# A transformer block on one core: a new order of work ahead of the first attention scores

## The chip, the core and the metric

The kernel runs on one core of a Trainium2 chip. The core has five instruction streams that work side by side and wait for one another through semaphores: TensorE (PE: matrix products and turns, with its weight loads shown as PEld), VectorE (DVE), ScalarE (ACT), GpSimd (POOL) and SyncE (SP), which here only issues DMA transfers. A suffix q (SPq, ACTq) marks an engine's own instruction sequencer, for instance while it issues a transfer. The metric is the device time of one execution in microseconds (us).

## The reference

Two sequences of 1024 tokens of width 256 go through self-attention, cross-attention to 154 condition tokens of width 192, and a gated feed-forward layer, with 16 heads of width 64, all in float32. Each stage starts with a layer norm and ends with a residual sum:

```python
h = _layernorm(x, ln1_g, ln1_b)
x = _attention(h, h, sa_wq, sa_wk, sa_wv, sa_wo, sa_bo) + x
h = _layernorm(x, ln2_g, ln2_b)
x = _attention(h, cond_emb, ca_wq, ca_wk, ca_wv, ca_wo, ca_bo) + x
h = _layernorm(x, ln3_g, ln3_b)
p = h @ ff_w1 + ff_b1
a, gate = (p[..., :D_FF], p[..., D_FF:])
h = a * jax.nn.gelu(gate, approximate=False) @ ff_w2 + ff_b2
return h + x
```

The change touches the first layer norm of the first sequence, and the first queries and keys that are made from it.

## The kernel before

Work on the first sequence begins with its 1024 tokens as eight tiles of 128 (`NT` = 8). `tile_order` pairs tile i with tile 4 + i, so the order is 0, 4, 1, 5, 2, 6, 3, 7. `norm_pieces` gives four lists of functions. `stats(t)` (L235) runs BATCH_NORM_STATS2 and its aggregation on DVE for the t-th tile of that order. `deviation(t)` (L245) makes 1/sqrt(var + eps) for a pair: a sum on DVE (L248), a power on POOL (L252). `normalize(t)` (L255) makes `off` = -mean x rstd on DVE (L258) and then the normalized pair `xn`, one tile on ACT (L276) and one on POOL (L273). `turn(t)` (L279) turns the pair on TensorE into two PSUM banks `ph` (two turns in each) and returns `store` (L290), which copies four chunks into `hT` with the norm's gain and shift, chunks 0 and 1 on DVE (L297), chunks 2 and 3 on ACT (L301). Gain and shift are columns of `cols`, one value for each partition.

Engines take their instructions in the order in which the program text emits them, since everything is under `tc.manual_schedule()` (L1264). So the lines 1290 to 1313 are a schedule written out by hand. `emit` (L1268) calls pieces one behind another. `part(what, i)` (L1279) projects 128 tokens of each half of the sequence to queries or keys of the first two heads (`project_both`, L362); the two halves go to two PSUM banks at once. `take(what, i)` (L1284) copies 256 such columns for each half into the tiles `q_sa` and `k_sa`, the first half on ACT, the second on DVE (`take_both`, L375). The names `own` and `banks` are the two double banks that later hold the first scores; `first_k` are two more banks for the last keys. 27 turns of the identity matrix (L1290) stand ahead of the first work of TensorE.

Behind that, the loop at L1324 runs 128 steps `p`. A step makes scores for two groups of 64 queries of one half against all 1024 keys (`self_first`, L704, and `scores`, L519), takes row maxima on DVE (L712) and exponents on ACT (L537), exchanges statistics between partitions by DMA (L547), and takes other pieces from the list `work` (`run_work`, L601), whose copies out of PSUM are held in `stores` until `flush(stores)` is called. Step 0 reads query columns 0 to 127 of the first half, step 1 columns 128 to 255. The queries that the beginning leaves out are the first entry of `work` (L1321): `self_queries(..., P, 2 * P)`, columns 256 to 511 of each half. Their copies to `q_sa` are both on ACT (L384).

Loads are issued on SP and ACT in the order of the text (L105 to L177): x's eight tiles in four transfers of two tiles, then gain and shift of the first norm straight into columns (L110, 4-byte elements), then the weights (L134), the other norms' parameters as rows (L172), the condition and a bias. Those rows are turned to columns by `turn_rows` (L192) during step 4. The transfers share eight semaphores; a ninth transfer is issued once the one before it on its semaphore has landed.

The pool `ps_m` gives the banks of `mm_tile`, `ps_o` those of `sum_tile`, two each. `held_v` (L214) holds values of the attention from step 1 on; its plane 3 is written by `move_values` (L449), which the loop calls first at step 5.

Of the kernel before, what the change touches and what calls it, by code (L numbers as in the profile page):

```python
# [13 lines left out]
P = 128  # L14
# [4 lines left out]
def tile_transformer_block(ctx: ExitStack, tc: tile.TileContext, a: dict, out: bass.AP):  # L19
# [63 lines left out]
    def load_x(queue, b, t):  # L83

        queue.dma_start(
            out=xt[b, t // GT][:, t % GT:t % GT + 2, :],
            in_=x[b, t * P:(t + 2) * P, :].rearrange("(t p) d -> p t d", p=P),
        )
# [125 lines left out]
    held_v = const.tile([P, 4, NT, P], F32, tag="held_v", name="held_v")  # L214
# [8 lines left out]
    def norm_pieces(kind, b, first=False):  # L223
# [21 lines left out]
        def deviation(t):  # L245
            mv = st["mv", t]
            var = small.tile([P, 2], F32, tag="var", name=f"var_{ln}_{b}_{t}")
            (nc.vector if first else nc.gpsimd).tensor_scalar(  # L248
                var, mv[:, :, 1], EPS, 1.0, op0=ALU.add, op1=ALU.mult
            )  # L250
            rstd = small.tile([P, 2], F32, tag="rstd", name=f"rstd_{ln}_{b}_{t}")
            nc.gpsimd.tensor_tensor(rstd, var, power, ALU.pow)  # L252
            st["rstd", t] = rstd

        def normalize(t):  # L255
            rstd = st["rstd", t]
            off = small.tile([P, 2], F32, tag="off", name=f"off_{ln}_{b}_{t}")
            nc.vector.scalar_tensor_tensor(  # L258
                off, st["mv", t][:, :, 0], -1.0, rstd, op0=ALU.mult, op1=ALU.mult
            )  # L260
# [8 lines left out]
            for i in range(2):  # L269
                xs = xt[b, order[t + i] // GT][:, order[t + i] % GT, :]  # L270
                xs, own = xs.rearrange("p (c d) -> p c d", c=nh), xn[:, :, i, :]
                if not narrow(kind, b) or first and i == 1:
                    nc.gpsimd.tensor_scalar(  # L273
                        own, xs, rstd[:, i:i + 1], off[:, i:i + 1], op0=ALU.mult, op1=ALU.add)
                else:
                    nc.scalar.activation(  # L276
                        own, xs, AF.Identity, bias=off[:, i:i + 1], scale=rstd[:, i:i + 1])

        def turn(t):  # L279

            n = 2 if first else 1
            bank = mm_tile if first and t == 2 else spare["bank"]
# [6 lines left out]

            def store():  # L290
                k = NC * 2 * P // nh
                for c in range(nh):
                    own = st["hT"][:, c, t // 2 * k:(t // 2 + 1) * k]
                    turned = ph[c * n // nh][:, c % (nh // n) * k:][:, :k]
                    gain, shift = cols[:, g0 + c:g0 + c + 1], cols[:, b0 + c:b0 + c + 1]
                    if spare["turned"] or first and c < nh // 2:
                        nc.vector.tensor_scalar(  # L297
                            own, turned, gain, shift, op0=ALU.mult, op1=ALU.add
                        )
                    else:  # L300
                        nc.scalar.activation(own, turned, AF.Identity, bias=shift, scale=gain)  # L301

            return store
# [960 lines left out]
    with tc.manual_schedule():  # L1264
# [19 lines left out]
        def take(what, i):  # L1284
            at = banks[what] if i < 2 else banks["k2"]
            take_both(qk["sa", 0, 0]["qk".index(what)], at, scale if what == "q" else None,
                      i * P, 2 * P, shared=True)


        for _ in range(27):  # L1290
            nc.tensor.transpose(own[0][:, 1, :P], ident, ident)
# [243 lines left out]
```

## Time and profile before

| what | value |
|---|---|
| time, median of 3 runs | 1073.81 us (1072.66 to 1074.61) |
| the profiled execution's own time | 1075.05 us |
| its span, first to last instruction | 1073.2 us |
| instructions | 48628 |
| granted TensorE clock, mean | 1.000 |
| DMA moved | 60.95 MB, mean 57 GB/s |

A row of the chain or the timeline begins with its start and its length in us. In groups and timelines there follow the engine, the line of the kernel (L526), the operation, and output<-input by the program's names; x32 is the number of instructions. A bracket at the end tells how long the engine was idle before and what it waited for. In a row of waits stands who waited for whom, the total in us, the number of times and the longest. A row of one tile's instructions has the shortest, median and longest duration in ns and the first and last start.

### The profile page before, as it was taken

The page shows a single profiled execution, that of the slowest core. Times are in us where ns is not written, and L with a number is a line of the kernel's source. Part 1 is how long each engine was busy: PE and PEld are TensorE (multiplying, and loading weights), DVE is VectorE, ACT ScalarE, POOL GpSimd, SP SyncE. Part 2 cuts the span into 40 slices and gives each one's busy share as a digit, 9 for nine tenths or more (in the row PEclk, how much of TensorE's full clock was granted, in tenths as well). Part 3 has the DMA queues.
Part 4 walks back from the last instruction along what each step waited for, and adds up shares of the span by engine and source line. Part 5 has one row for each costly group of instructions (what it writes and reads, how often), then busy time and mean ns, then how long its engine had stood idle before and what let it go on. Part 6 is the DMA issues. An engine that isn't in the chain of part 4 may idle for free.

```text
span 1073.2 us, 48628 instructions
## 1 busy us (share of the span) xinstructions
PE 1059.4 (99%) x20196; PEld 716.2 (67%) x20196; DVE 883.1 (82%) x1321; ACT 646.9 (60%) x2096; POOL 777.0 (72%) x1652
## 2 busy tenths in 40 slices
PE   8999999999999999999999999999999999999998
PEld 6566777556556555555665665466766667788998
DVE  5789899998989989999999899968777887655554
ACT  5766677677666666676777666665566564342231
POOL 2677777778777777677777777776666876499884
PEclk9999999999999999999999999999999999999999
DMA  3132122121021121111111101125776545000000
GB/s 101 38 73 54 29 68 53 25 63 41 22 59 25 34 51 34 39 34 34 44 22 45 44 14 38 36 59 139 164 177 172 123 108 114 16 6 15 21 10 30
DMA packets 86045, 60.95 MB, mean 57 GB/s; under 512 B 32122, under 2 KB 74562, under 8 KB 85826
## 3 DMA queue, kind: packets, MB, share of 16 engines
q1 hardware_dynamic: 84450, 57.07, 22.1%
q8 instruction: 159, 2.61, 1.1%
q10 hardware_dynamic: 1376, 0.79, 0.2%
q14 instruction: 60, 0.49, 0.2%
HBM read 27.91 MB, written 2.10 MB: 28 GB/s over the span
## 4 chain that ended last, share of the span: by engine, by line
PE 74%; DMA 7%; SPq 6%; POOL 6%; DVE 2%; issue 2%; ACT 1%; POOLq 0%; DVEq 0%; ACTq 0%
PE s L526 14%; PE po L578 13%; DMA st<-st 7%; SPq L547 6%; PE py_ca L500 5%; PE py_sa L500 4%; PE poc L951 4%; PE pq_ca L369 4%; PE pq_sa L369 4%; PE pb L1072 4%; PE pk_sa L369 4%; PE pq L1217 3%; PE pv_sa L405 3%; POOL p L650 3%; PE sc L871 2%; PE pa L1072 2%
## 5 line engine op out<-in xcount | busy, mean ns | idle before, releaser
L650 POOL TENSOR_SCALAR p<-p,rd,ee 128x512 f32<-128x512 f32 x512 | 391.9, 771 | 80.0 <-DVE rd L640 79.6
L537 ACT ACTIVATE p<-s,st 128x512 f32<-128x512 f32 x512 | 345.5, 687 | 169.7 <-DVE st L712 164.5
L712 DVE TENSOR_REDUCE st<-s 128x2 f32<-128x1024 f32 x256 | 308.6, 1206 | 56.8 <-issue 17.3
L675 DVE STREAM_TRANSPOSE pT<-p 128x1024 f32<-128x1024 f32 x256 | 302.8, 1219 | 1.5 <-POOL p L650 1.2
L526 PE MATMUL s<-k_sa,q_sa 64*32 64x512 f32 x4096 | 257.8, 591 | 2.8 <-ACT p L537 2.0
L578 PE MATMUL po<-pT,held_v 64*32 64x256 f32 x8192 | 240.8, 376 | 0.7 <-DVE pT L675 0.6
L578 PEld LDWEIGHTS po<-pT,held_v 64*32 64x32 f32 x8192 | 182.5, 106 | 67.0 <-issue 26.0
L526 PEld LDWEIGHTS s<-k_sa,q_sa 64*32 64x32 f32 x4096 | 89.7, 106 | 93.1 <-issue 46.6
L888 ACT ACTIVATE p<-sc,neg 128x154 f32<-128x154 f32 x256 | 96.4, 405 | 78.9 <-DVE rden L896 75.0
L899 POOL TENSOR_SCALAR p<-p,rden 128x154 f32<-128x154 f32 x256 | 97.3, 406 | 51.8 <-DVE rden L896 51.5
L537 ACT ACTIVATION_READ_ACCUMULATOR p<-s,st 128x1 f32 x512 | 104.0, 203 | 0.0
L555 POOL TENSOR_TENSOR dd<-st 128x8 f32<-128x8 f32 x128 | 26.0, 203 | 82.4 <-DMA st<-st 80.6
L500 PE MATMUL py_sa<-sa_wo,o_sa 128*128 128x256 f32 x256 | 59.7, 386 | 1.0 <-ACT held_v L415 1.0
L500 PE MATMUL py_ca<-ca_wo,o_ca 128*128 128x256 f32 x256 | 60.2, 383 | 0.0
L877 DVE TENSOR_REDUCE neg<-sc 128x6 f32<-128x924 f32 (+1 forms) x48 | 47.8, 996 | 14.9 <-PE sc L871 14.9
L369 PE MATMUL pq_ca<-hT_ln,ca_wq 64*64 64x512 f32 (+1 forms) x544 | 59.1, 590 | 0.9 <-DMA ca_wq<-in_L_xattn_ca_wq_dram 0.8
L500 PEld LDWEIGHTS py_sa<-sa_wo,o_sa 128*128 128x128 f32 x256 | 47.3, 190 | 19.0 <-issue 5.2
L369 PE MATMUL pq_sa<-hT_ln,sa_wq 64*32 64x512 f32 (+1 forms) x976 | 57.8, 586 | 0.7 <-ACT held_v L415 0.7
L369 PE MATMUL pk_sa<-hT_ln,sa_wk 64*32 64x512 f32 x960 | 57.1, 590 | 0.2 <-ACT q_sa L384 0.2
L888 ACT ACTIVATION_READ_ACCUMULATOR p<-sc,neg 128x1 f32 x256 | 56.5, 221 | 0.0
L915 DVE STREAM_TRANSPOSE pT_ca<-p 128x480 f32<-128x480 f32 (+1 forms) x96 | 52.9, 587 | 0.9 <-POOL p L899 0.8
L405 PE MATMUL pv_sa<-sa_wv,hT_ln 64*32 64x256 f32 x1792 | 52.9, 376 | 0.0
(158 smaller groups left out, 1476.0 us busy)
## 6 DMA issues: line engine op xcount, KB each, us to landing
wf<-pT_ca SPq DMA_DIRECT2D x128, 128.0 KB, 2.4
st<-st SPq DMA_DIRECT2D x512, 1.0 KB, 2.0
held_v<-held_v SPq DMA_DIRECT2D x32, 256.0 KB, 4.0
sa_wq<-in_L_xattn_sa_wq_dram SPq DMA_DIRECT2D x32, 128.0 KB, 2.8
sa_wk<-in_L_xattn_sa_wk_dram SPq DMA_DIRECT2D x32, 128.0 KB, 3.6
sa_wv<-in_L_xattn_sa_wv_dram SPq DMA_DIRECT2D x16, 256.0 KB, 4.2
ca_wq<-in_L_xattn_ca_wq_dram SPq DMA_DIRECT2D x32, 128.0 KB, 3.1
wf<-in_L_xattn_ff_w_dram SPq DMA_DIRECT2D x12, 256.0 KB
```

The source lines that it names most:

```text
L369: nc.tensor.matmul(pq[r][f:f + m, at:at + n], lhsT=wt[own, c, f:f + m], rhs=h[own, c, t0:t0 + n], start=(c == 0), stop=(c == NH - 1), tile ...
L405: nc.tensor.matmul(pv[r][f:f + KB, e * VC:(e + 1) * VC], lhsT=h[half, c, t0:t0 + KB], rhs=wt[half, c, :], start=(c == 0), stop=(c == NH - ...
L500: nc.tensor.matmul(py[:, e * D:(e + 1) * D], lhsT=o[:, i, (t + e) * P:(t + e + 1) * P], rhs=wo[kind][:, g * HP + i, :], start=(i == 0), st ...
L526: nc.tensor.matmul(sc[a4 * KB:(a4 + 1) * KB, j, :], lhsT=q[r, c:c + KB], rhs=k[r, h * HB:(h + 1) * HB], start=True, stop=True, tile_positi ...
L537: nc.scalar.activation(pr[:, j, :], sc[:, j, :], AF.Exp, bias=st[:, 0, 0, i, j:j + 1], accum_out=st[:, 0, 1, i, j:j + 1],)
L578: nc.tensor.matmul(po[a2][d:d + KB, :QH // 2], lhsT=v[e][r, t, d:d + KB], rhs=pT[r, d // DH * NK + n, :], start=(t == 0 and e == 0), stop= ...
L650: nc.gpsimd.tensor_scalar(pr[:, j, :], pr[:, j, :], own["rd"][:, c:c + 1], own["ee"][:, 0, c:c + 1], op0=ALU.mult, op1=ALU.mult,)
L675: nc.vector.transpose(halves[h][:, :, c:c + KB], slots[p]["p"][i].rearrange("p j (n k) -> p (j n) k", k=KB))
L712: nc.vector.tensor_reduce(st[:, 0, 0, i, :], sc[i], AX.X, ALU.max, negate=True)
L888: nc.scalar.activation(pr_[:, j, i, :T], sc[:, j, i * T:(i + 1) * T], AF.Exp, bias=neg[:, j, i:i + 1], accum_out=den[:, j, i:i + 1],)
L899: nc.gpsimd.tensor_scalar(pr_[:, j, i, :T], pr_[:, j, i, :T], rden[:, j, i:i + 1], 1.0, op0=ALU.mult, op1=ALU.mult,)
L1072: nc.tensor.matmul(into[:, :BT], lhsT=lhs, rhs=wh[pair][i], start=first, stop=True, skip_group_check=True)
```

## The change

It does these things, all ahead of the scores of step 1.

- x's first four tiles are loaded as single tiles, then gain and shift of the first norm as eight rows (in a plane of `held_v` that isn't used yet, hence the earlier allocation), then x's last four tiles in two transfers.
- The eight rows are turned by TensorE and copied to `cols` on ACT.
- In the first norm, `off` is made by POOL from a negated mean that DVE makes. Of the second pair both tiles are normalized on POOL.
- Statistics stand ahead of the chunk copies in DVE's order; `turn` returns a function that copies one chunk on the engine named, and the list tells which. Turns 0 and 2 use the banks of `sum_tile`, turns 1 and 3 those of `mm_tile`.
- 20 turns of the identity instead of 27 ahead, and 5 more behind turn 0.
- All four key parts go to one bank for each half; of the queries, part 0 alone is made ahead of the first scores, and `self_queries` makes columns 128 to 511 behind them. Their copies are flushed at the end of step 0.

```diff
-    def load_x(queue, b, t):
+    def load_x(queue, b, t, n):
         queue.dma_start(
-            out=xt[b, t // GT][:, t % GT:t % GT + 2, :],
-            in_=x[b, t * P:(t + 2) * P, :].rearrange("(t p) d -> p t d", p=P),
+            out=xt[b, t // GT][:, t % GT:t % GT + n, :],
+            in_=x[b, t * P:(t + n) * P, :].rearrange("(t p) d -> p t d", p=P),
         )
...
-    for t in range(0, NT // 2, 2):
-        load_x(nc.sync, 0, t)
-        load_x(nc.scalar, 0, NT // 2 + t)
-    for n in names[:2]:
-        for r0 in range(0, P, HR):
-            (nc.scalar if n == names[0] else nc.sync).dma_start(
-                out=cols[r0:r0 + HR, row_of[n]:row_of[n] + NH],
-                in_=w[n].rearrange("(r p) -> p r", p=HR),
-            )
+    for t in range(2):
+        load_x(nc.sync, 0, t, 1)
+        load_x(nc.scalar, 0, NT // 2 + t, 1)
+    held_v = const.tile([P, 4, NT, P], F32, tag="held_v", name="held_v")
+    rows1 = held_v[:n_cols, 3, 0, :]
+    for n, queue in zip(names[:2], (nc.scalar, nc.sync)):
+        own = rows1[row_of[n]:row_of[n] + NH, :]
+        for f in range(0, P, HR):
+            queue.dma_start(out=own[:, f:f + HR], in_=w[n].rearrange("(r p) -> r p", p=HR))
+    load_x(nc.sync, 0, 2, 2)
+    load_x(nc.scalar, 0, NT // 2 + 2, 2)
...
             st["rstd", t] = rstd
+            if first:
+                neg = small.tile([P, 2, 4], F32, tag="zz", name=f"neg_{ln}_{b}_{t}")[:, 0, :2]
+                nc.vector.tensor_scalar(neg, mv[:, :, 0], -1.0, 1.0, op0=ALU.mult, op1=ALU.mult)
+                off = st["off", t] = small.tile([P, 2], F32, tag="off", name=f"off_{ln}_{b}_{t}")
+                nc.gpsimd.tensor_tensor(off, neg, rstd, ALU.mult)
...
-                if not narrow(kind, b) or first and i == 1:
+                if not narrow(kind, b) or first and (i == 1 or t == 2):
                     nc.gpsimd.tensor_scalar(
...
-            bank = mm_tile if first and t == 2 else spare["bank"]
+            bank = mm_tile if first and t % 4 == 2 else spare["bank"]
...
+            def store_chunk(c, vector):
+                k = NC * 2 * P // nh
+                own = st["hT"][:, c, t // 2 * k:(t // 2 + 1) * k]
+                turned = ph[c * n // nh][:, c % (nh // n) * k:][:, :k]
+                gain, shift = cols[:, g0 + c:g0 + c + 1], cols[:, b0 + c:b0 + c + 1]
+                if vector:
+                    nc.vector.tensor_scalar(own, turned, gain, shift, op0=ALU.mult, op1=ALU.add)
+                else:
+                    nc.scalar.activation(own, turned, AF.Identity, bias=shift, scale=gain)
...
         def part(what, i):
-            at = banks[what] if i < 2 else banks["k2"]
-            project_both(at, wsl["sa", 0, what], hT["sa", 0], P, i * P, P, i % 2 * P)
+            project_both(banks[what], wsl["sa", 0, what], hT["sa", 0], P, i * P, P, i * P)
...
-        for _ in range(27):
-            nc.tensor.transpose(own[0][:, 1, :P], ident, ident)
-        emit(stats[0], stats[1], deviation[0])
-        emit(stats[2], stats[3], normalize[0], deviation[1], stats[4], normalize[1])
-        copies = [turn[0](), turn[1]()]
-        copies[0]()
+        warm(own[0][:, 1], 20)
+        emit(stats[0], stats[1], deviation[0], stats[2], normalize[0], stats[3], deviation[1], stats[4])
+        nc.tensor.transpose(own[1][:, 0, :n_cols], rows1, ident[:n_cols, :n_cols])
+        nc.scalar.copy(cols[:, :n_cols], own[1][:, 0, :n_cols])
+        turned = [turn[0]()]
+        warm(own[0][:, 1], 5)
+        chunks(turned[0], (0,), (1, 2, 3))
+        emit(normalize[1])
         part("q", 0)
+        turned.append(turn[1]())
         part("k", 0)
-        emit(stats[5], deviation[2])
-        copies[1]()
-        emit(stats[6], normalize[2], stats[7], deviation[3])
-        copies = turn[2]()
-        part("q", 1)
+        emit(stats[5], deviation[2], stats[6])
+        chunks(turned[1], (), (2, 3))
+        emit(normalize[2], stats[7], deviation[3])
+        chunks(turned[1], (0, 1), ())
+        turned.append(turn[2]())
+        part("k", 1)
         emit(normalize[3])
-        copies()
-        part("k", 1)
-        copies = turn[3]()
-        banks["k2"] = two_banks("first_k")
+        chunks(turned[2], (0, 1), (2, 3))
+        take("q", 0, 1)
+        turned.append(turn[3]())
         part("k", 2)
-        copies()
-        take("q", 0)
-        take("k", 0)
+        chunks(turned[3], (0, 1), (2, 3))
         part("k", 3)
-        take("k", 2)
+        take("k", 0, 2)
+        take("k", 2, 2)
...
-        work.append(costing(2, lambda: self_queries(*units[0], P, 2 * P)))
+        work.append(costing(2, lambda: self_queries(*units[0], P, P)))
...
+            if p == 0:
+                flush(stores)
```

`chunks(store_chunk, vector, scalar)` calls the copy of each chunk of its first list on DVE, then of its second list on ACT; `warm(bank, n)` turns the identity n times; the third argument of `take` is the number of 128-column blocks.

More of the change, by code (lines that the diff above doesn't have):

```diff
@@ L213, in tile_transformer_block @@
     ends = const.tile([P, DA // 2], F32, tag="ends", name="ends")
-    held_v = const.tile([P, 4, NT, P], F32, tag="held_v", name="held_v")
     hT, vs, qk, oT = {}, {}, {}, {}
@@ L253, in deviation @@
             st["rstd", t] = rstd
+            if first:
[3 more added lines that the diff above has]
+                nc.gpsimd.tensor_tensor(off, neg, rstd, ALU.mult)
         def normalize(t):
             rstd = st["rstd", t]
[L257 to L260, printed above, removed]
+            if first:
+                off = st["off", t]
+            else:
+                off = small.tile([P, 2], F32, tag="off", name=f"off_{ln}_{b}_{t}")
+                nc.vector.scalar_tensor_tensor(
+                    off, st["mv", t][:, :, 0], -1.0, rstd, op0=ALU.mult, op1=ALU.mult
+                )
             if narrow(kind, b) and not first:
@@ L288, in turn @@
                     st["xn", t][i], ident)
+            def store_chunk(c, vector):
[5 more added lines that the diff above has]
+                    nc.vector.tensor_scalar(own, turned, gain, shift, op0=ALU.mult, op1=ALU.add)
+                else:
+                    nc.scalar.activation(own, turned, AF.Identity, bias=shift, scale=gain)
             def store():
-                k = NC * 2 * P // nh
                 for c in range(nh):
[L293 to L303, printed above, removed]
+                    store_chunk(c, spare["turned"])
+            return store_chunk if first else store
         return (
@@ L1279, in part, with take @@
         def part(what, i):
-            at = banks[what] if i < 2 else banks["k2"]
-            project_both(at, wsl["sa", 0, what], hT["sa", 0], P, i * P, P, i % 2 * P)
-        def take(what, i):
-            at = banks[what] if i < 2 else banks["k2"]
+            project_both(banks[what], wsl["sa", 0, what], hT["sa", 0], P, i * P, P, i * P)
+        def take(what, i, n):
+            at = [bank[:, i * P:] for bank in banks[what]]
             take_both(qk["sa", 0, 0]["qk".index(what)], at, scale if what == "q" else None,
-                      i * P, 2 * P, shared=True)
@@ L1290, in tile_transformer_block, with chunks @@
-        for _ in range(27):
-            nc.tensor.transpose(own[0][:, 1, :P], ident, ident)
-        emit(stats[0], stats[1], deviation[0])
-        emit(stats[2], stats[3], normalize[0], deviation[1], stats[4], normalize[1])
-        copies = [turn[0](), turn[1]()]
-        copies[0]()
+                      i * P, n * P, shared=True)
+        def chunks(store_chunk, vector, scalar):
+            for c in vector:
+                store_chunk(c, True)
+            for c in scalar:
+                store_chunk(c, False)
@@ new lines, in warm @@
+        def warm(bank, n):
+            for _ in range(n):
+                nc.tensor.transpose(bank[:, :P], ident, ident)
+        warm(own[0][:, 1], 20)
[5 more added lines that the diff above has]
+        chunks(turned[0], (0,), (1, 2, 3))
```

## The prediction

> **What bounds the kernel now.** I read the page's busy row and chain first, then what TensorE waits for (whole span, and 17 to 80 us), and then only the beginning.
>
> ```profile
> PE 1059.4 (99%) x20196; PEld 716.2 (67%) x20196; DVE 883.1 (82%) x1321; ACT 646.9 (60%) x2096; POOL 777.0 (72%) x1652
> ...
> PE 74%; DMA 7%; SPq 6%; POOL 6%; DVE 2%; issue 2%; ACT 1%; POOLq 0%; DVEq 0%; ACTq 0%
> ...
> PE first L1291 <- POOL ident masks.py:199: 1.9, 1, 1.9
> PE ph_ln L286 <- POOL xn_ln L273: 1.5, 5, 0.8
> ...
> PE s L526 <- DVE k_sa L390: 0.6, 1, 0.6
> PE pk_sa L369 <- ACT q_sa L384: 0.2, 1, 0.2
> ```
>
> TensorE is busy 1059.4 of 1073.2 us. The last two rows are all that it waits for between 17 and 80 us. So a microsecond counts only if TensorE's own sequence reaches the same instruction earlier; what other engines gain is worth nothing. Now the beginning: the chain, TensorE's timeline, and busy time per stretch (the first figure is its length, the second TensorE's):
>
> ```profile
> 1.91 6.02 PE first L1291 x27
> 7.93 0.45 PE ph_ln L286 x4
> ...
> 15.09 2.03 PE first_k L369 x32
> ...
> 17.71 1.95 PE s L526 x32
> 19.67 1.93 PE pq_sa L369 x16
> 21.59 0.67 PE pc L203 x8
> ...
> 22.19 1.96 PE L526 MATMUL s<-k_sa,q_sa 64*32 64x512 f32 x32
> ...
> 22.19:49.00 26.81, 26.81 (x426) 14.91 (x425) 19.34 (x21) 20.35 (x63) 14.82 (x33) 1.00 0.13 31
> ```
>
> Up to 7.7 us TensorE turns the identity. First scores (p=0) start at 17.71, those of p=1 at 22.19; from there TensorE is busy 26.81 of 26.81 us, and the change alters nothing behind it. **The ruler is therefore the start of p=1's scores, 22.19 us**, not that of the first scores.
>
> **The change part by part.** *x and the first statistics.*
>
> ```profile
> 4.33 0.43 DVE L242 BATCH_NORM_STATS2 st_ln<-x 128x6 f32<-128x256 f32 x1 [4.33 <-DMA x<-in_x_dram]
> ...
> 4.89 0.40 DVE L242 BATCH_NORM_STATS2 st_ln<-x 128x6 f32<-128x256 f32 x1
> ...
> 5.53 0.17 DVE L248 TENSOR_SCALAR var_ln<-mv_ln 128x2 f32<-128x2 f32 x1
> ...
> 5.78 0.71 POOL L252 TENSOR_TENSOR rstd_ln<-var_ln,power 128x2 f32<-128x2 f32 x1 [3.93 <-DVE var_ln L248]
> 6.92 0.56 POOL L273 TENSOR_SCALAR xn_ln<-x,rstd_ln,off_ln 128x256 f32<-128x256 f32 x1 [0.43 <-DVE off_ln L258]
> ...
> GB/s 0 19 141 378 386 127 65 213 233 231 231 83 8 104 198 192 87 0 0 0 0 0 0 0 18 1 1 1 149 115 10 1 138 126 1 18 0 0 0 0
> ...
> SPq L134 <- DMA x<-in_x_dram: 1.8, 2, 1.5
> 4.64 1.26 SPq L134 DMA_DIRECT2D sa_wq<-in_L_xattn_sa_wq_dram  x2
> ```
>
> The GB/s row (window 0 to 40 us) has one figure per microsecond: 0.16 MB had moved by 3 us, 378 KB/us follow. The first two loads (0.51 MB) were through at about 3.9; statistics began at 4.33 and SP's wait for x ended at 4.64, so landing lags by 0.4 to 0.7. With single tiles the first pair (0.26 MB) is through at 3.25 and lands at 3.65 to 3.95; I let tile 4's statistics start at 4.1 instead of 4.89. Bounds: no gain (the lag rules, not the bytes) to 0.8. The wait of the weight load, ninth transfer in order, falls on x's last pair in the new order: issued at about 4.1, landing near 6.5, where the fifth statistics want them at 6.3. On ACT's queue this issue (0.5) and the table load (row below, 1.28) stand ahead of the first normalization: ready at 5.9, just in time; 0.3 late if tile 4 lands at 4.4.
>
> *First normalization.* Before, 4.89 to 7.48 (POOL's 6.92 + 0.56). After: 0.81 to the variance's end, 0.08 + 0.71 for the power, `off` on POOL, 0.60 on ACT. POOL's price for a small product is its 128x8 row:
>
> ```profile
> 27.90 0.20 POOL L555 TENSOR_TENSOR dd<-st 128x8 f32<-128x8 f32 x1 [14.40 <-DMA st<-st]
> ...
> 4.38 1.28 ACT L276 ACT_TABLE_LOAD   x1 [4.38 <-DMA x<-in_x_dram]
> 6.85 0.60 ACT L276 ACTIVATE xn_ln<-x,off_ln,rstd_ln 128x256 f32<-128x256 f32 x1 [1.19 <-DVE off_ln L258]
> ...
> L1291 PE MATMUL first<-ident x27: 418/421/472, 1.9 to 7.5; 128*128 128x128 f32 x27
> ...
> L286 PE MATMUL ph_ln<-ident,xn_ln x16: 272/273/327, 7.7 to 14.8; 128*128 128x128 f32 x16
> L297 DVE TENSOR_SCALAR hT_ln<-ph_ln,cols x8: 400/404/410, 8.4 to 15.2; 128x128 f32<-128x128 f32 x8
> L301 ACT ACTIVATE hT_ln<-ph_ln,cols x8: 439/446/457, 8.9 to 15.5; 128x128 f32<-128x128 f32 x8
> ```
>
> The negation (about 0.15) runs on DVE beside the power and costs nothing; without that cover, 0.15. Sum 2.55, so xn is ready at 6.65 instead of 7.48: 0.83 gained.
>
> *Warm-up, rows, first turn.* 27 turns of the identity start 0.215 apart; 20 end at 6.2. The row turn follows (to 6.45; at most one slow turn); its four small loads stand ahead of x's last pair and should land before 5 us (ff_b1's rows took 2.2 us, the old element-wise columns 5.1):
>
> ```profile
> cols<-in_L_xattn_ln_g_dram ACTq DMA_DIRECT2D x2, 1.0 KB, 5.1
> rows<-in_L_xattn_ff_b_dram SPq DMA_DIRECT2D x1, 8.0 KB, 2.2
> ```
>
> Were they later than 6.65, TensorE would stand. A turn takes 421 ns until 7.5 us and 273 from there: TensorE changes to full speed at about 7.8. I keep that moment. Turn 0 then runs slowly (4 x 0.215, 6.75 to 7.6), and of the five new turns one is slow and four are fast (0.12, from the 0.66 below for four): 8.3. Copies: three on ACT, 0.35 apart, 7.45 to 8.65; one on DVE, behind the fifth statistics, to 7.85. q0 starts at 8.3, and its last quarter needs the copy of 8.65: no wait. A 128-column part takes 1.0 up to the next (k2 and k3 together 2.06):
>
> ```profile
> 9.68 1.16 PE L369 MATMUL first<-hT_ln,sa_wq 64*128 64x128 f32 x16
> ...
> 14.43 0.66 PE L286 MATMUL ph_ln<-ident,xn_ln 128*128 128x128 f32 x4
> 14.91 0.73 DVE L297 TENSOR_SCALAR hT_ln<-ph_ln,cols 128x128 f32<-128x128 f32 x2 [1.43 <-PE ph_ln L286]
> 15.01 2.06 PE L369 MATMUL first_k<-hT_ln,sa_wk 64*128 64x128 f32 x32
> ```
>
> So q0 ends at 9.3. Weights: nothing new ahead of them but 2 KB; taken to be there.
>
> *The rest up to the first scores.* POOL has the second pair by 8.85 (behind its own 0.56 to 6.65: power, `off`, two normalizations, a gap before each), so turn 1 runs 9.3 to 9.85, k0 to 10.85. ACT: two copies to 10.7, normalization 2 to 11.25. Turn 2 11.35 to 11.9 (TensorE stood 0.5), k1 to 12.9, turn 3 to 13.45, k2 and k3 to 15.5. Then the takes:
>
> ```profile
> 17.14 0.42 DVE L390 COPY k_sa<-first_k 128x256 f32<-128x256 f32 x1 [0.85 <-PE first_k L369]
> ```
>
> k0's take now shares a bank with k3, and is issued behind it. Turn 3's copy started 0.48 behind the first of its turns, where one turn lasts 0.33: it waited for the second in its bank. If k0's does too, two copies in a row cost 0.33 more (else nothing). First scores: 15.5 + 0.33 + 0.42 + 0.14 (17.71 less the copy's end) = **16.4, 1.3 earlier**.
>
> *128 queries behind the first scores.* TensorE loses 1.0 ahead of the scores and gains it behind (1.93 for 256 columns, 2.9 for 384): nothing in sum. But p=1 now reads columns that are copied on ACT only behind p=0's four exponents; flushing there is what the last edit does.
>
> ```profile
> 20.22 0.69 ACT L537 ACTIVATE p<-s,st 128x512 f32<-128x512 f32 x1 [2.75 <-DVE st L712]
> ...
> 22.89 0.67 ACT L384 ACTIVATE q_sa<-pq_sa 128x256 f32<-128x256 f32 x2
> ...
> L384 ACT ACTIVATE q_sa<-pq_sa 128x512 f32<-128x512 f32 x2 | 1.1, 598 | 0.0
> L384 ACT ACTIVATE q_sa<-pq_sa 128x256 f32<-128x256 f32 x2 | 0.7, 400 | 0.0
> ```
>
> The copy starts 5.18 behind the first scores (22.89 - 17.71); 384 columns lie between 400 and 598 ns, 0.50; 0.1 to TensorE: p=1 at +5.78. TensorE itself is there at 1.95 + 2.9 + 0.67 = +5.5, so it stands 0.3, and all of its queue (values, context keys) with it. Before, the step was 4.48. **p=1: 16.4 + 5.78 = 22.18 against 22.19**: nothing gained, or 0.33 if k0's take doesn't wait. No row decides between the two; I take the middle, 0.17. Of 1.3 us won at the first scores, the copy behind the exponents takes nearly all back.
>
> The profiled run took 1075.05 (span 1073.2), which becomes 1074.88; it lay 1.2 above the median of the runs, 1073.81 (1072.66 to 1074.61). So 1073.6.
>
> [...]
>
> **Rivals.**
>
> 1. *The head's gain survives* (1073.0). Full speed comes half a microsecond earlier, so turn 0 and the five turns save 0.45, and k0's take hides: first scores 15.6, p=1 21.4, 0.8 earlier. For it: 0.3 of TensorE's stand is soft. Against: the exponents' 5.18 stays whatever comes earlier.
> 2. *Single tiles land hardly earlier* (1074.1). The lag rules; tile 4 at 4.6: p=1 is 0.45 later than forecast, 22.5. For it: statistics started 0.4 behind the bytes.
> 3. *TensorE stays slow* (1075.0), slower than before. Before, its work was unbroken from 1.91 to 8.36. Now it stands between the row turn (6.45) and turn 0 (6.75). [...] If it takes 5.8 us anew from 6.75, as from 1.91 to 7.7, everything up to k1 is slow: 2.6, 1076.2. Against: the gap is short, 0.3 us.
>
> [...]
>
> **How the numbers follow.** Forecast 0.43; rival 1 0.23; rival 2 0.14; rival 3 0.15 (0.10 at 1075.0, 0.05 at 1076.2); the rest, that something unseen moves over 2 us either way, 0.05. About 0.2%, 2.15 us, is what can be told from no change: 1071.66 to 1075.96. Faster has half of the rest and rival 1's tail with the spread of a median, 0.08; slower half of the rest, rival 3's far end and a tail, 0.09; same 0.83. The range takes in rivals 1 and 2 and the near rival 3 with half a microsecond of spread: 1071.9 to 1075.4.
>
> **What would show it.** Statistics at about 3.6, xn by 6.7, first scores at 16.1 to 16.4; TensorE's waits get a new row, scores on ACT's `q_sa` copy, 0.3; p=1 near 22.0. Wrong it would be if turns or q0 still show 421 ns behind 8.3 us, if the row turn waits for DMA, if p=1 starts before 21.3 or after 23, or if the chain behind p=1 isn't 27 us of unbroken TensorE.

## The result, and the profile after

| | median us | lowest to highest | runs |
|---|---|---|---|
| before | 1074.61 | 1072.40 to 1075.57 | 13 |
| after | 1077.22 | 1074.55 to 1080.57 | 13 |

The changed kernel is slower: ratio 1.0026, 95% interval 1.0015 to 1.0036, which is 1.6 to 3.9 us. Forecast was no difference. The profiled execution of the changed kernel took 1074.78 (span 1073.0), near the low end of its own runs, so the two spans alone (1073.2 and 1073.0) don't show the loss; it has to be looked for in rows that repeat from profile to profile. The page of after:

```profile
PE 1060.0 (99%) x20179; PEld 716.8 (67%) x20179; DVE 882.7 (82%) x1320; ACT 645.9 (60%) x2097; POOL 775.9 (72%) x1657
...
q8 instruction: 159, 2.61, 1.0%
...
PE 90%; DVE 4%; DMA 1%; POOL 1%; ACT 1%; issue 1%; SPq 1%; DVEq 0%; ACTq 0%; POOLq 0%
```

TensorE has 17 products less than before (20196). (Here and below a product is one record of TensorE: a product of the program makes two records, a turn one; the 8 products more of a_split and the 16 turns more of a_pad16 below both bring 16, 20195 against 20179.) The second row is one that I hadn't weighed: 159 packets with 2.61 MB, 16 KB each, on a DMA queue of the kind "instruction", the first at 14.4 us and the last at 1057.8. I read them as code that is fetched while the kernel runs. Spread over TensorE's 20179 products and as many weight loads they are 65 bytes for each, so I read them as TensorE's program, some 250 instructions to a packet by this estimate.

The beginning of after, TensorE's timeline (lines above 300 are ten higher than before):

```profile
6.37 0.27 PE L1310 MATMUL first<-ident,held_v 8*128 8x8 f32 x1
6.57 0.66 PE L295 MATMUL ph_ln<-ident,xn_ln 128*128 128x128 f32 x4
7.06 0.71 PE L1306 MATMUL first<-ident 128*128 128x128 f32 x5
7.73 0.46 PE L379 MATMUL first<-hT_ln,sa_wq 64*128 64x128 f32 x2
8.81 1.13 PE L379 MATMUL first<-hT_ln,sa_wq 64*128 64x128 f32 x14 [0.63 <-ACT hT_ln L307]
9.87 0.66 PE L295 MATMUL ph_ln<-ident,xn_ln 128*128 128x128 f32 x4
...
12.00 0.63 PE L295 MATMUL ph_ln<-ident,xn_ln 128*128 128x128 f32 x4 [0.38 <-ACT xn_ln L285]
...
14.24 2.06 PE L379 MATMUL first<-hT_ln,sa_wk 64*128 64x128 f32 x32
17.27 1.95 PE L536 MATMUL s<-k_sa,q_sa 64*32 64x512 f32 x32 [0.98 <-DVE k_sa L400]
19.15 2.85 PE L379 MATMUL pq_sa<-hT_ln,sa_wq 64*128 64x384 f32 x16
21.93 0.74 PE L205 MATMUL pc<-ident,cn 77*96 77x77 f32 x8
22.93 1.09 PE L536 MATMUL s<-k_sa,q_sa 64*32 64x512 f32 x16 [0.26 <-ACT q_sa L394]
```

Up to turn 0 nearly all is a little earlier than forecast (the row turn ends at 6.64, forecast 6.45). Then q0 starts, stands and ends at 9.87, where I had 9.3; first scores come at 17.27 (before 17.71, forecast 16.4), p=1 at 22.93 (before 22.19, forecast 22.18). So 0.74 is lost where I looked. The rest of the 2.6 is lost where I had said that the change alters nothing. The sum of TensorE's busy time from 23 us to the end, for before and for after (the second figure is TensorE's, the count stands behind it):

```profile
23.00:1080.00 1057.00, 1039.83 (x19993) 700.34 (x19985) 871.72 (x1284) 636.56 (x2073) 770.73 (x1636) 1.00 0.23 55
```

```profile
23.00:1080.00 1057.00, 1041.17 (x20001) 702.50 (x20001) 871.21 (x1284) 635.05 (x2071) 768.43 (x1636) 1.00 0.23 55
```

After takes 1.3 us longer. About 0.5 of it is eight products of step 1 that before, being earlier, had done ahead of 23 us (32 take 1.95); the rest is the same work. The waits that the profile lists for TensorE don't show it. I read it as small stands that the profile counts as busy time; step 34 below has one, where 64 query products take 3.94 instead of 3.64. But the span behind p=1 is no longer in this profile of after than in that of before (1050.1 and 1051.0), and the sum of busy time scatters from profile to profile: counted for the same 20001 products, it lies between 1038.6 and 1041.4 in the first nine profiles of the table at the end of the experiments and between 1041.2 and 1042.3 in its last four. One pair of such rows, here and below, is a sign and not a measure of the loss.

### The profile page after: what moved, and what is told of

The parts are those of the page before. It is cut to its first block, busy times and chain, and to the rows that moved or that the text cites. A ratio compares the mean times of both kernels' runs of the same rounds, so it can differ in the third digit from the quotient of the medians.

```text
span 1073.0 us, 48602 instructions
## 1 busy us (share of the span) xinstructions
PE 1060.0 (99%) x20179; PEld 716.8 (67%) x20179; DVE 882.7 (82%) x1320; ACT 645.9 (60%) x2097; POOL 775.9 (72%) x1657
## 3 DMA queue, kind: packets, MB, share of 16 engines
q8 instruction: 159, 2.61, 1.0%
## 4 chain that ended last, share of the span: by engine, by line
PE 90%; DVE 4%; DMA 1%; POOL 1%; ACT 1%; issue 1%; SPq 1%; DVEq 0%; ACTq 0%; POOLq 0%
PE po L588 20%; PE s L536 20%; PE py_sa L510 5%; PE py_ca L510 5%; PE pk_sa L379 5%; PE pq_sa L379 4%; PE pv_sa L415 4%; PE pq_ca L379 4%; PE pb L1082 4%; PE poc L961 4%; PE pq L1227 3%; PE pa L1082 2%; PE sc L881 2%; PE pc L1082 2%; PE pf L1257 1%; PE ph_ln L295 1%
```

## The experiments

Eleven runs, in three groups. The kernel before ran beside each group, with medians of 1074.38 (first four), 1074.29 (next four) and 1073.40 (last three); each ratio is against the one beside it.

**1. The changed kernel again (a_again).** No edit.

> The changed kernel once more, for a second profile and more times. Its first profile starts step 1's scores at 22.93 us, 0.74 later than before, with TensorE at full speed from 6.6 us, and yet its own time, 1074.78, is among the lowest of 13 (median 1077.22). Gate theory (in most executions full speed comes late, since turns are fewer and followed by gaps): this profile shows 421 ns instructions behind 8.3 us and step 1 at 24 or later whenever its time is above 1077. Weights theory (query products wait for the second half of sa_wq, landed at 8.68): full speed before 8.3 us and step 1 within 22.6 to 23.3, whatever the time. Downstream theory (stalls behind step 1 differ from execution to execution): same start, and the difference in time arises at single steps behind p=5.

1077.25, ratio 1.0027 (1.0013 to 1.0040). The loss is there a second time. In its profile TensorE has the full clock from 5.59 us on and p=1 is at 23.01, 0.81 later than before, much as in the first and as the weights theory has it (22.6 to 23.3).

**2. Before with 20 turns (b_20).**

```diff
-        for _ in range(27):
+        for _ in range(20):
```

> The kernel before with 20 turns of the identity ahead instead of 27, nothing else. [...] Weights and downstream theories: within 0.7 us of before.

1075.16, ratio 1.0015 (1.0001 to 1.0029). Its busy time by stretch (the column behind POOL is the granted clock) and TensorE's timeline:

```profile
5.70:9.00 3.30, 1.04 (x8) 0.59 (x6) 2.49 (x12) 1.23 (x3) 2.48 (x4) 1.00 0.64 156
9.10:12.40 3.30, 3.28 (x24) 2.97 (x26) 2.63 (x12) 1.97 (x5) 1.66 (x3) 0.50 0.65 160
12.50:23.00 10.50, 9.86 (x135) 7.32 (x134) 5.06 (x10) 4.52 (x13) 0.73 (x2) 1.00 0.18 55
```

```profile
7.60 0.63 PE L286 MATMUL ph_ln<-ident,xn_ln 128*128 128x128 f32 x4 [1.48 <-POOL xn_ln L273]
9.12 1.09 PE L286 MATMUL ph_ln<-ident,xn_ln 128*128 128x128 f32 x4 [0.89 <-POOL xn_ln L273]
10.13 2.08 PE L369 MATMUL first<-hT_ln,sa_wq 64*128 64x128 f32 x16
```

TensorE stood for 1.48 and 0.89 and then had half the clock from 9.07 to 12.49: q0 took 2.08 instead of 1.16, first scores and p=1 came 1.38 later. That is the mechanism of my third rival, but not of the changed kernel: there turn 0 took 0.66 and no product behind it is slow.

**3. The changed kernel with 27 turns ahead (a_27).**

```diff
-        warm(own[0][:, 1], 20)
+        warm(own[0][:, 1], 27)
```

> The changed kernel with 27 turns ahead instead of 20. Gate theory: full speed by 7.8 to 8.5 us as before, 1 to 2.5 us faster than the changed kernel. Weights theory: turn 0 moves from 6.6 to about 7.8, its copies end 1.0 later, past the weights: same to 1.0 us slower than the changed kernel. Downstream theory: same as the changed kernel within 0.7.

1076.29, ratio 1.0022 (1.0010 to 1.0033); p=1 at 22.98. The clock isn't what the change lost by.

**4. The changed kernel without its edit of the queries (a_queries).**

```diff
         turned.append(turn[2]())
+        part("q", 1)
         part("k", 1)
...
-        take("q", 0, 1)
+        take("q", 0, 2)
...
-        work.append(costing(2, lambda: self_queries(*units[0], P, P)))
+        work.append(costing(2, lambda: self_queries(*units[0], P, 2 * P)))
...
-            if p == 0:
-                flush(stores)
```

> The changed kernel with 256 queries of each half ahead of the first scores again (second query part, take of 256, self_queries from column 256, no flush at the end of step 0). By the profile of the changed kernel step 1 starts 5.66 behind the first scores, and 4.48 before: the 128 queries cost 5.66 - 4.48 - 1.0 = 0.18 us. Weights and gate theories: same as the changed kernel within 0.7, step 1's scores 0.1 to 0.3 earlier, at 22.7. A third theory, that the queries moved cost more than their wait (ACT's copies of 384 columns and a late flush upset the steps behind): 1 to 2.5 us faster than the changed kernel.

1074.87, ratio 1.0005 (0.9996 to 1.0015): most of the loss is gone. Yet p=1 starts at 22.90, only 0.03 earlier than in the changed kernel (first scores 18.42, 1.15 later; the step 4.48 instead of 5.66). The edit of the queries costs some 2 us, and not at the beginning.

Step by step, the starts of the scores then showed single steps that were longer in the three profiles of the changed kernel and its 27 turns than in the others; those that I followed hung on the exchange of statistics. Step 34 in TensorE's, POOL's and ACT's timeline, before:

```profile
197.12 1.92 PE L526 MATMUL s<-k_sa,q_sa 64*32 64x512 f32 x32
198.83 3.64 PE L369 MATMUL pq_sa<-hT_ln,sa_wq 64*32 64x512 f32 x64
202.27 1.06 PE L526 MATMUL s<-k_sa,q_sa 64*32 64x512 f32 x16
...
196.88 0.20 POOL L555 TENSOR_TENSOR dd<-st 128x8 f32<-128x8 f32 x1
...
197.58 1.18 ACT L415 COPY held_v<-pv_sa 128x256 f32<-128x256 f32 x4
```

and in the changed kernel again:

```profile
197.79 1.92 PE L536 MATMUL s<-k_sa,q_sa 64*32 64x512 f32 x32
200.04 3.94 PE L379 MATMUL pq_sa<-hT_ln,sa_wq 64*32 64x512 f32 x64 [0.33 <-ACT held_v L425]
203.50 1.02 PE L536 MATMUL s<-k_sa,q_sa 64*32 64x512 f32 x9
...
198.40 0.20 POOL L565 TENSOR_TENSOR dd<-st 128x8 f32<-128x8 f32 x1 [1.62 <-DMA st<-st]
...
199.09 1.17 ACT L425 COPY held_v<-pv_sa 128x256 f32<-128x256 f32 x4
```

Read it from below: ACT empties the value banks, in which the next queries go, behind the exponent `ee`; that waits for POOL's `dd`, and that for the exchange. Before, `dd` starts 0.24 ahead of the scores; here 0.61 behind them, having waited 1.62 for the DMA. The copies come 0.84 later against the scores (1.30 instead of 0.46), the queries 0.54, and the step is 5.71 instead of 5.15.

Why is the exchange late? The last of its four transfers of 1 KB completes in 16 shares, one by one (the page counts 16 DMA engines). At step 34, in twelve of the 13 profiles below, fifteen of the 16 are in at 1.1 to 1.5 ahead of the scores; the sixteenth follows the end of a 16 KB code fetch by 1.1 to 1.4 us, so I read that it sat behind that packet on one engine. The traces' records of single packets bear this out: each of the four transfers moves as 32 packets of 32 bytes, and in after, a_again, a_27 and b_queries 30 of the last transfer's packets start within 0.16 us of one another, 1.65 to 1.94 ahead of the scores, while the other two start within 0.02 us of the fetch's end, 0.6 to 1.0 ahead. Where the fetch falls decides.

Hence a new theory, **the fetch theory**: the change takes TensorE instructions out ahead of step 1 (the queries go from 128 and 256 columns in two sets of 16 products to 384 in one), each later line of code is wanted at another point of its step, and some fetches fall on the last transfer of an exchange that TensorE's banks hang on. Its rival is that the wait on the late query copy, and what it displaces, is what costs.

**5 and 6. Small turns that do nothing (a_pad16, a_pad8).** Ahead of q0, where TensorE stands anyway:

```diff
         emit(normalize[1])
+        for _ in range(16):
+            nc.tensor.transpose(own[0][:8, 1, :8], ident[:8, :8], ident[:8, :8])
         part("q", 0)
```

with 8 in the other.

> The changed kernel with 16 turns of 8 columns (8x8 of the identity) on TensorE ahead of the first query product, in the stand in which it waits for the query weights until 8.8 us: they are to cost nothing at the head and only put 16 products and 16 weight loads more into TensorE's code, about as many as the edit of the queries took out (some 2 KB, an eighth of one 16 KB code fetch). Fetch theory (the fewer instructions shift each later 16 KB code fetch by some 0.6 us against its step, onto the exchange that TensorE waits for): p=1 stays at 22.9, the extra stalls at the steps 5 to 6 and 34 to 35 go (6.1 and 5.2 instead of 6.6 and 5.5), the fetches start 2.6 ahead of those steps instead of 2.0, and the time falls to 1074.6 to 1075.4. Queries theory (the wait on the late query copy and what it displaces at p=1 is what costs): as the changed kernel, 1077.0 to 1077.5.

> As the one with 16 small turns, with 8. Fetch theory: half the shift, a time in between (about 1076), as with the seven more turns ahead (1076.3). Queries theory: 1077.0 to 1077.5.

16: 1075.04, ratio 1.0007 (0.9997 to 1.0018). 8: 1074.94, ratio 1.0008 (0.9997 to 1.0019). p=1 stays at 22.87 and 22.96. Sixteen useless turns of 8 columns win back 2 us of the 2.6, while everything up to p=1, the wait on the query copy too, is as in the changed kernel. The queries theory falls. Eight do as much as 16: the time in between that I expected for 8 was wrong, the effect is not in proportion. Step 34 with 16 turns:

```profile
196.28 1.98 PE L536 MATMUL s<-k_sa,q_sa 64*32 64x512 f32 x32
198.12 3.94 PE L379 MATMUL pq_sa<-hT_ln,sa_wq 64*32 64x512 f32 x64
201.57 1.31 PE L536 MATMUL s<-k_sa,q_sa 64*32 64x512 f32 x13
...
196.47 0.20 POOL L565 TENSOR_TENSOR dd<-st 128x8 f32<-128x8 f32 x1 [0.86 <-DMA st<-st]
...
197.16 1.18 ACT L425 COPY held_v<-pv_sa 128x256 f32<-128x256 f32 x4
```

and its busy time behind 23 us:

```profile
23.00:1080.00 1057.00, 1039.04 (x20001) 697.35 (x19995) 871.20 (x1284) 634.59 (x2071) 768.55 (x1636) 1.00 0.23 55
```

The same 20001 products as in the changed kernel take 2.1 us less, within the scatter named above.

**7. The late queries as two products (a_split).**

```diff
-        work.append(costing(2, lambda: self_queries(*units[0], P, P)))
+        def rest_queries():
+            pq = two_banks("pq_rest")
+            project_both(pq, wsl["sa", 0, "q"], hT["sa", 0], P, P, P)
+            project_both(pq, wsl["sa", 0, "q"], hT["sa", 0], P, 2 * P, 2 * P, P)
+            return lambda: take_both(qk["sa", 0, 0][0], pq, scale, P, 3 * P)
+        work.append(costing(2, rest_queries))
```

> The changed kernel, its 384 query columns behind the first scores as two products, of 128 and of 256 columns, into the same two banks and with the same copy: the order of the work, the waits and the copy stay, TensorE has 8 products more in its program (16 of its instructions and 16 weight loads). Fetch theory: 1074.6 to 1075.6, p=1 at 22.9 to 23.1, the steps 5 to 6 and 34 to 35 short again. Queries theory: 1077.0 to 1077.7.

1074.99, ratio 1.0007 (0.9996 to 1.0017); p=1 at 22.89. The same from another place: the instructions come back behind the first scores, with the same columns, copy and wait.

**8. Before with the edit of the queries alone (b_queries).**

```diff
         copies = turn[2]()
-        part("q", 1)
...
-        take("q", 0)
+        take("q", 0, 1)
...
-        work.append(costing(2, lambda: self_queries(*units[0], P, 2 * P)))
+        work.append(costing(2, lambda: self_queries(*units[0], P, P)))
...
+            if p == 0:
+                flush(stores)
```

> The kernel before with the edit of the queries alone: 128 columns ahead of the first scores, 384 behind them, the waiting copies emptied behind the first step. Everything else is the kernel before. At the head I expect first scores about 1.0 earlier and p=1 at 22.0 to 22.5. Fetch theory: 16 instructions fewer (and 16 weight loads) put the fetches onto the exchange here too: 1 to 2.5 slower than the kernel before, 1075.4 to 1077. Queries theory: the wait at p=1 costs as much as in the changed kernel, 1076.5 to 1077. If neither holds, and the loss comes from the head alone: within 0.5 of the kernel before.

1077.01, ratio 1.0024 (1.0012 to 1.0035). The kernel before gets the loss too. Both theories allowed for such a time; that the fetches move as the fetch theory has it (table below) speaks for that one. The beginning went otherwise than I expected: first scores 17.33, only 0.38 earlier, and p=1 at 23.05, 0.86 later. Behind 23 us:

```profile
23.00:1080.00 1057.00, 1042.33 (x20001) 690.42 (x20001) 871.47 (x1284) 635.34 (x2071) 768.41 (x1636) 1.00 0.23 55
```

2.5 us more than before, 2.0 without the eight products of step 1; it is the highest of the 13 profiles.

**9 and 10. The beginning (a_rows, a_best).** Both with the 16 small turns. First the parameters with one transfer each:

```diff
-        for f in range(0, P, HR):
-            queue.dma_start(out=own[:, f:f + HR], in_=w[n].rearrange("(r p) -> r p", p=HR))
+        queue.dma_start(
+            out=own.rearrange("r (f p) -> r f p", p=HR),
+            in_=w[n].rearrange("(r p) -> r p", p=HR).unsqueeze(1).to_broadcast([NH, 2, HR]))
```

and, in a_best, beside it:

```diff
-            project_both(banks[what], wsl["sa", 0, what], hT["sa", 0], P, i * P, P, i * P)
+            at = banks["q" if i > 1 else what]
+            project_both(at, wsl["sa", 0, what], hT["sa", 0], P, i * P, P, i * P)
...
-        chunks(turned[0], (0,), (1, 2, 3))
+        chunks(turned[0], (0, 1), (2, 3))
...
+        take("k", 0, 2)
         part("k", 2)
         chunks(turned[3], (0, 1), (2, 3))
         part("k", 3)
-        take("k", 0, 2)
         take("k", 2, 2)
```

(`take` reads the same banks as `part`.)

> The changed kernel with the 16 small turns, its first norm's parameters loaded with one transfer each (the 64 values read twice into a row) instead of two: SP and ACT each issue one transfer less ahead of x's last pair and of the weights, which come some 0.6 earlier. Weights theory (q0's stand until 8.8 on the second half of the query weights is what the head lost): q0 ends 0.5 earlier, first scores at 16.7 and p=1 at 22.4. Rival, normalization theory (turn 2 waits for POOL's third normalization until 12.0 whatever q0 does): q0 ends earlier, TensorE stands longer ahead of turn 2, and p=1 gains only what the earlier x gives the statistics, 22.6 to 22.9. Time by both within 0.6 of the 1075.0 of the kernel with the 16 small turns.

> As a_rows, and turn 0's copies two on DVE and two on ACT (one bank each); the last two key parts go to the free columns of the query banks, so that the first keys are taken behind the second key part and not behind the last, two copies in a row. TensorE's instructions are the same in number and order. Bank theory: one take less in front of the first scores, 0.4 earlier than in a_rows; p=1 at 22.0 to 22.5; time 1074.0 to 1074.8, about the kernel before. If the first take delays turn 3's copies instead, nothing is gained: first scores as in a_rows.

a_rows: 1075.18, ratio 1.0017 (1.0008 to 1.0026). a_best: 1074.88, ratio 1.0010 (1.0000 to 1.0021). TensorE in a_rows:

```profile
8.23 1.68 PE L380 MATMUL first<-hT_ln,sa_wq 64*128 64x128 f32 x16
9.85 0.66 PE L296 MATMUL ph_ln<-ident,xn_ln 128*128 128x128 f32 x4
...
11.98 0.63 PE L296 MATMUL ph_ln<-ident,xn_ln 128*128 128x128 f32 x4 [0.38 <-ACT xn_ln L286]
...
17.24 1.95 PE L537 MATMUL s<-k_sa,q_sa 64*32 64x512 f32 x32 [0.97 <-DVE k_sa L401]
```

and in a_best:

```profile
8.33 1.40 PE L380 MATMUL first<-hT_ln,sa_wq 64*128 64x128 f32 x16
9.67 0.66 PE L296 MATMUL ph_ln<-ident,xn_ln 128*128 128x128 f32 x4
...
11.80 0.63 PE L296 MATMUL ph_ln<-ident,xn_ln 128*128 128x128 f32 x4 [0.38 <-ACT xn_ln L286]
...
16.93 1.95 PE L537 MATMUL s<-k_sa,q_sa 64*32 64x512 f32 x32 [0.61 <-DVE k_sa L401]
```

The starts of q0's 16 products in after and in a_rows, and what they could wait for:

```
        q0's products, start us                          weights' 2nd half   x's last tiles   ACT's copies
after   7.73 7.92 | 8.81 8.82 9.00 ... 9.56 9.67         landed 8.68         6.06, 6.93       7.57 to 8.73
a_rows  8.23 8.45 8.52 8.71 8.73 8.82 8.94 ... 9.64 9.64  landed 8.39         7.20, 7.47       8.22 to 9.38
```

With the weights in at 8.39 the stand is gone, yet q0 ends no earlier. The last tiles of x, though one transfer less stands ahead of them on each queue (the key weights behind them on SP were issued at 5.04, in after at 5.57), landed later, at 7.20 and 7.47 instead of 6.06 and 6.93; the fifth statistics and DVE's chunk 0 stood behind them, ACT's copies behind that chunk, and q0's products now keep the pace of the copies. So the weights held q0 in after, and the copies are right behind them. p=1 is at 22.91: the weights theory's 22.4 is missed, the other's 22.6 to 22.9 met but for 0.01. In a_best the first scores are 0.31 earlier than in a_rows; the stand ahead of them is 0.61 instead of 0.97, one copy less in a row, as the bank theory has it. p=1 comes at 22.59, short of the expected 22.5, and still 0.40 behind before; the time, too, is just above the expected 1074.0 to 1074.8. Neither version beats the kernel before, and no other did.

**11. Before with the 16 small turns (b_pad16).**

```diff
-        copies = [turn[0](), turn[1]()]
+        copies = [turn[0]()]
+        for _ in range(16):
+            nc.tensor.transpose(own[0][:8, 1, :8], ident[:8, :8], ident[:8, :8])
+        copies.append(turn[1]())
```

> The kernel before with 16 turns of 8 columns in the 0.76 us in which TensorE waits for the second normalization: 32 instructions and loads more, which moves the code fetches the other way from the change, further ahead of their steps. Fetch theory: p=1 unchanged at 22.2, steps 34 to 35 and 90 to 91 at 5.15, fetches some 3.3 ahead of them; the time within 0.6 of the kernel before, 1073.8 to 1074.9, since the exchange is already clear; it would be wrong if any move of the fetches, in either direction, costs 2 us.

1074.44, ratio 1.0007 (0.9997 to 1.0017), p=1 at 22.16. The move the other way brings the fetches further ahead (3.8 and 3.1) and costs nothing that can be told.

All profiles side by side. Times of fetches and completions in us from the start of the step's scores; "behind p=1" is the ratio's loss in us less the delay of p=1:

```
            TensorE   --- step 34 -------------------  step 90        p=1    loss   behind
            products  fetch  15th   16th  step length  fetch  length  delay  total  p=1
b_pad16     20212     -3.83    *      *      5.15      -3.10   5.15   -0.04   0.8    0.8
before      20196     -2.60  -1.38  -0.47    5.15      -2.60   5.15     -      -      -
a_queries   20195     -2.81  -1.42  -0.17    5.15      -2.10   5.15    0.70   0.5   -0.2
a_pad16     20195     -2.45  -1.09   0.03    5.29      -2.35   5.15    0.67   0.8    0.1
a_split     20195     -2.78  -1.43  -0.44    5.15      -2.58   5.15    0.70   0.8    0.1
a_rows      20195     -2.69  -1.34  -0.30    5.15      -2.50   5.15    0.72   1.8    1.1
a_best      20195     -2.71  -1.43  -0.48    5.15      -2.57   5.15    0.40   1.1    0.7
b_20        20189     -2.68  -1.50  -0.09    5.23      -2.03   5.18    1.38   1.6    0.2
a_pad8      20187     -2.67  -1.42  -0.50    5.15      -2.18   5.15    0.77   0.9    0.1
a_27        20186     -2.12  -1.42   0.17    5.44      -1.91   5.35    0.79   2.4    1.6
b_queries   20180     -2.16  -1.46   0.23    5.55      -1.86   5.53    0.86   2.6    1.7
after       20179     -1.97  -1.29   0.22    5.48      -1.72   5.35    0.74   2.8    2.1
a_again     20179     -1.56  -1.42   0.45    5.71      -1.71   5.69    0.81   2.9    2.1
* the fetch holds an earlier transfer of the exchange there
```

Nine profiles with 20187 products and more have steps of 5.15 to 5.29 at step 34 and lose on average 0.4 us behind p=1 (before counted as none: 0.3); four with 20186 and fewer have 5.44 to 5.71 and lose 1.9. Each loss is uncertain by some 1.1 us, the groups as a whole by less. The edge between 20187 and 20186 is sharp: at step 34 the fetch jumps by half a microsecond there. Why it jumps was not tried. No kernel takes 16 products out of the kernel before without moving the queries.

## Why the prediction was wrong, point by point

*Where it failed most:* "the change alters nothing behind it. The ruler is therefore the start of p=1's scores, 22.19 us". The ruler measured only 0.74 of the loss. A stretch without gaps says that TensorE waits for nothing up to 49 us, not that a shift of its code leaves the next thousand alone: of the small stands behind 23 us the list of waits shows next to none, since, as I read the profile, they lie in busy products. I had counted the products that the edit of the queries removes ahead of the scores and adds behind them as columns ("nothing in sum"); as instructions they don't come back. That they decide is shown by experiments 5 to 8: added in two places, two microseconds go; taken out of the kernel before together with the move of the queries, they come. That the fetch delays the exchange is shown in the completions of steps 34 and 90. These two steps carry 0.3 and 0.2 us each in the first profile of after and 0.6 and 0.5 in the second. Step 62 is a third such place: in the last four rows' profiles the last two packets of the exchange start within 0.02 us of a fetch's end, the sixteenth share completes 0.53 to 0.89 behind the scores (in the other nine profiles 0.30 at the latest), and the step is 6.56 to 6.92 long (6.17 to 6.55). From the start of p=1 to that of the last step, the four profiles take on average 1.7 us longer than the nine, uncertain by some 0.8; steps 34, 62 and 90 carry 0.37, 0.29 and 0.33 of it, 1.0 in all. Where the rest lies stays open. It isn't the same rule everywhere: step 5, which I first took for such a place (6.03 before, 6.53 to 6.69 in the changed kernel), is 6.63 in a_best and 5.84 in b_queries.

*"Weights: nothing new ahead of them but 2 KB; taken to be there."* They weren't: the second half landed at 8.68. It had landed at 8.61 before, when q0 came only at 9.68; the prediction shows no row for that landing. Each product of the program is two records, so q0's third record is the first product with the weights' second half; it wants no chunk but 0, which DVE had done at 7.53, and it starts at 8.81. In a_again, a_27, a_queries, a_pad8 and a_split, too, q0's third record starts 0.13 to 0.14 behind that landing (8.64 to 8.93). The profile puts the stand down to ACT's copies, because the last of these ends at 8.73:

```profile
7.57 1.16 ACT L307 ACTIVATE hT_ln<-ph_ln,cols 128x128 f32<-128x128 f32 x3 [0.73 <-DVE hT_ln L305]
```

```profile
7.12 0.41 DVE L305 TENSOR_SCALAR hT_ln<-ph_ln,cols 128x128 f32<-128x128 f32 x1 [0.39 <-PE ph_ln L295]
```

The copies themselves came when forecast (7.45 to 8.65), ACT's first waiting for DVE's in the same bank. q0 ends 0.57 late, turn 1 and ACT's copies with it, the third normalization on ACT stands behind these, and so turn 2 is at 12.00 instead of 11.35. k3 ends 0.8 late: the 1.3 us that I expected at the first scores became 0.44.

*Right:* xn was ready at 6.41 (forecast 6.65); from the start of tile 4's statistics that is 2.54, against a forecast of 2.55. The terms that the forecast names add up to only 2.40, since it calls the negation's 0.15 covered; two gaps around `off`, 0.19 in all, made up for it. k0's take does wait for k3's bank: two copies stand in a row ahead of the first scores, 0.98 in all, and taking one away gave 0.31 (forecast 0.33). p=1 follows the first scores by 5.66 (forecast 5.78), with TensorE standing 0.26 for ACT's `q_sa` (forecast 0.3). With the other edits in place, the edit of the queries is even at p=1 (22.90 without, 22.87 to 22.96 with it), as forecast.

*The rivals.* The third (TensorE stays slow) would have been nearest in time, for a wrong reason: the changed kernel's turns and products are fast from 6.57 on. No run shows what its 1075.0 rests on; in its place b_20 showed half the clock from 9.07 to 12.49 and a price of 1.38 at p=1. The first had its cause right, full speed from turn 0 on, and its gain was lost at q0. The moment of full speed, which the forecast kept at 7.8, moves from profile to profile: it lies between 5.36 and 7.83 us in the 13, and at 6.56 and 5.59 in two profiles of the same changed kernel. None of the nine profiles of the changed kernel and its versions falls back to half the clock ahead of the end; whether executions without a profile do, no run shows. The second didn't come: the first statistics started at 3.31 instead of 4.33 and tile 4's at 3.87 instead of 4.89, so the tile-wise loads brought 1.0. The 4.6 that this rival takes for tile 4 lay within the prediction's bounds, 4.1 to 4.89, but no run shows it.

The sum by terms: beginning, forecast -0.17, measured +0.74; everything behind p=1, forecast 0, measured some 2. Forecast 1073.6, measured 1077.2; of these 3.6, 0.8 lies in the start, since the kernel before has a median of 1074.61 in its 13 runs and had 1073.81 in the three that the forecast started from. The signs of being wrong that the prediction set watch only the first 50 us; p=1, at 22.93 and in the second profile at 23.01, lies at its limit of 23.

## What to carry to other kernels

Where one engine is busy 99%, a difference of 2 us in 1074 can be the position of its code (behind p=1 four profiles here lose 1.9 us on average, nine 0.4): before an edit gets the credit or the blame, put the instructions that it removed back as ones that do nothing, at a place where the engine stands. Compare the starts of the same step from profile to profile and follow the longer ones back to a transfer; sums over a span hide them. An edit that saves something at the start pays only if no second wait holds the same instruction: here q0 hung on its weights (landed at 8.68), and right behind them on copies (the last ended at 8.73).

## What the runs showed of the hardware

A 16 KB fetch of code lasts 0.9 to 1.4 us (steps 34 and 90 of all profiles). A share of a 1 KB transfer that waits for it (two packets of 32 bytes, which start as the fetch ends) completes 1.0 to 1.4 us behind the fetch's end, while the other fifteen shares had been in for 0.8 to 1.9 us. That both use the same DMA engine is read from this; the traces don't name the engine. The packet is not free for the transfers beside it: at steps 34, 62 and 90 it goes with 1.0 of the 1.7 us above. POOL's `dd` started behind the last share, not behind the fifteenth: in step 34 of the changed kernel again fifteen were in at -1.42, the last at 0.45, and `dd` started at 0.61.

The half clock in b_20 lasted 3.4 us (9.07 to 12.49). Ahead of it, from 5.70 to 9.00, TensorE was busy for 1.04 of 3.30 us at a granted clock of 1.00; behind it, from 12.50 to 23.00, for 9.86 of 10.50 at 1.00 again.
